# A four-layer graph network on one core: a negated sigmoid gate, one selection per stretch, and a stream of adjacency pieces in other memory

## The chip, the cores and the metric

The kernel runs on one core of a Trainium2 chip. The core has four compute engines with a queue each: TensorE (PE: matrix products; its weight loads are listed as PEld), VectorE (DVE), ScalarE (ACT) and GpSimd (POOL). SyncE (SP) computes nothing here and issues most of the transfers. Every engine works through its own instructions in order and waits for others through semaphores. Transfers between HBM and the on-chip memory run on 16 DMA engines, whichever queue issued them.

The metric is the device time of one execution in microseconds. Before the change it is 3158.1 us, the median of 17 runs between 3150.41 and 3168.55.

## What is computed

There are 3125 nodes with 128 features, and 50000 edges sorted by destination. Four graph layers follow each other, each with a residual and a layer norm:

```python
edge_index = jnp.stack([src, dst])
x = _layernorm(x + _L0_gnn_ref(x, edge_index, edge_weight, ...))      # 3 GCN layers with relu
x = _layernorm(x + _L1_gnn_ref(x, edge_index, ...))                   # GATv2 attention, 4 heads
x = _layernorm(x + _L2_gnn_ref(x, edge_index, edge_attr_128, ...))    # CGConv
x = _layernorm(x + _L3_gnn_ref(x, edge_index, edge_weight, ...))      # 10 GCN layers, LN, GELU, residual
```

Each GCN layer computes D^-1/2 (A + I) D^-1/2 (x W) + b. The part that the change rewrites most is layer 2, which works on edges:

```python
z = jnp.concatenate([x[dst], x[src], edge_attr], axis=-1)
gate = jax.nn.sigmoid(z @ W_f + b_f)
core = jax.nn.softplus(z @ W_s + b_s)
agg = jax.ops.segment_sum(gate * core, dst, num_segments=x.shape[0])
return x + agg
```

## The kernel before, in words

**Dense products (layers 0 and 3).** The kernel builds the dense adjacency matrix in HBM, as 7 banks of 460 columns by 25 row tiles of 128. A GCN layer is then a product of the node features with these banks. `Convolutions.sums` (line 657 loads, line 691 multiplies) goes over a bank in pieces of five row tiles, 128x5x460 floats or 1150 KB each. Some pieces stay on chip (`adj`), the others pass through a stream of buffers (`adj_k`). Five matmuls use one piece. When the 25 matmuls of a bank are done, its sums are evicted to `aggT`, and a later product with the layer's weights (`po`, line 708) gives the new rows.

**Layer 0 and the building of the adjacency.** `l0_sorted` builds the banks from one-hot matrices on PE (`heavy`, `side`), collects each bank in a `strip`, stores it (line 562), and runs the first GCN layer from the strips on the way. Two memory pools serve this: `l0_strips` and `l0_hot` (the one-hots), opened in this order. When they are closed, the stream `l0_adj` with four buffers and `l0_hold` take their place; a tile in memory that others used must wait for the last reader of those. Then `load_nodes` (line 147) loads x again and `Attention.prepare` (lines 1077 to 1137) loads and computes the index tables of layer 1: zeros stored to HBM, the padded destinations `dst_pad`, `wide`, `order`, `src_o`. All these transfers are on SP's queue, as are the pieces `adj_k`.

**Layer 1** goes over the edges in 28 stretches of 14 chunks of 128 edges. A stretch has four blocks, of 4, 4, 3 and 3 chunks (`BLOCKS`). For each chunk POOL gathers 128 rows by an indirect transfer (line 217). The gathered rows of a stretch are one tile `xj`, with six buffers.

**Layer 2** (`l2_sorted`, from line 1362) first computes two tables, one row per node (lines 1440 to 1470): `to_src`, the product with the source part of the weights, and `to_dst`, that with the destination part plus the bias, in three bf16 parts. `w2` and `b2` hold the weights and biases of gate (index 0) and core (index 1). Then it goes over the same 28 stretches:

- `load(s)`: SP loads `xw` (the stretch's own node rows), POOL gathers the fourteen chunks of `zj`, a tile per stretch, three buffers.
- `load_block(s, b)`: SP loads `td` (42 consecutive rows of `to_dst`, three parts each), `eaT` (edge features) and `drow` (each edge's local destination, broadcast over 126 partitions), four blocks ahead.
- `select(s, b)`: DVE compares `drow` with the partition's number, which gives the one-hot `of_node`, two blocks ahead.
- `products(s, b)`: PE multiplies `eaT` by the weights and `of_node` by `td`, into `pz` in PSUM (three buffers).
- `soften`: DVE adds `zj` (z = pz + zj), ACT takes Abs. `soften_more`: ACT takes Exp(−|z|), then Ln(1 + that), back into `pz`.
- `gate_core`: DVE computes min(z, 0) − ln for the gate, ACT its Exp; DVE computes max(z, 0) + ln for the core.
- `messages`, `place`: DVE multiplies gate and core to `msg`, and builds the one-hot `of_edge`.
- `add_up(s)`: PE sums the messages by node, one matmul per chunk, and adds the carried part of the stretch before (`agg`, by `shift`). `rows(s)` copies the sums to `agg`, forms u = 2·xw + agg and its moments; `finish(s)` writes the normalised rows y and stores them to `after`.

While this goes on, layer 3's first GCN layer begins. After stretches 6, 12, 18 and 24 (`WHOLE`), `fetch` loads finished rows of x back and `scale` multiplies them by dinv on ACT. From stretch 7 on, each stretch takes one adjacency piece `adj_u` (`load_unit`, three buffers): `unit` multiplies it with five matmuls at the end of the stretch (b = 3), and `add_unit` adds the sums to `aggT` at the start of the next (b = 0). The last seven units come after the last stretch.

**Layer 3** then starts with its first product's remaining rows (the last five row tiles), with loads of bias and norm rows (`three`, line 1701, three buffers) on SP ahead of its pieces.

**The order of the work.** In layer 2 the order on PE, DVE, ACT and SP is written out: `InOrder` (helper, line 181, which records every instruction under line 189) chains each instruction to the one before on its engine. The loop at lines 1634 to 1675 steps through all blocks, k = 4s + b, and calls the functions above for different blocks at each step. Only POOL's gathers and the operations outside of `InOrder` are placed by the scheduler.

Of the kernel before, what the change touches and what calls it, by code (L numbers as in the profile page):

```python
# [18 lines left out]
P = 128  # L19
D = 128  # L20
# [28 lines left out]
def tile_gnn_stack(ctx: ExitStack, tc: tile.TileContext, a: dict, out: bass.AP):  # L49
# [96 lines left out]
    def load_nodes():  # L146
        nc.sync.dma_start(x, a["x"].rearrange("(t p) d -> p t d", p=P))
# [635 lines left out]
    def l0_sorted(edges, adj, attention):  # L783


        with (
# [13 lines left out]
            with (  # L800
                tc.tile_pool(name="l0_strips", bufs=2) as strips,
                tc.tile_pool(name="l0_hot", bufs=2) as hot,
            ):
                lanes.pin()
                edges.build(strips, hot, ps, adj, lambda b, strip: conv.sums(x, b, *layers[0], strip), ready)
                lanes.free()
            with (
# [3 lines left out]
                load_nodes()  # L811
# [249 lines left out]
    class Attention:  # L1061
# [15 lines left out]
        def prepare(self, scratch, ps, ve):  # L1077
# [11 lines left out]
            nc.sync.dma_start(self.left[NP:].rearrange("p a b -> p (a b)"), zero)  # L1089
            zero_f = scratch.tile([P, D], F32, name="zero_f")  # L1090
            nc.vector.memset(zero_f, 0.0)
            nc.sync.dma_start(self.before[NP:], zero_f)
            nc.sync.dma_start(self.after[NP - P:NP], zero_f)
            nc.sync.dma_start(self.logits[:, :NEAR], zero_f[:HEADS, :NEAR])
            nc.sync.dma_start(self.logits[:, NEAR + NCH * P:], zero_f[:HEADS, :NEAR])
            edge = scratch.tile([1, NEAR + 1], I32, name="edge")
            nc.vector.memset(edge, NP)
            nc.sync.dma_start(dst_pad[:, :NEAR + 1], edge)
            nc.sync.dma_start(dst_pad[:, NEAR + 1 + NCH * P:], edge)
            v = a["dst_r"]  # L1100
            nc.sync.dma_start(dst_pad[:, NEAR + 1:NEAR + 1 + NCH * P],
# [4 lines left out]
            nc.sync.dma_start(wide, bass.AP(tensor=dst_pad.tensor, offset=dst_pad.offset,  # L1106
# [6 lines left out]
            nc.sync.dma_start(order, bass.AP(tensor=v.tensor, offset=v.offset,  # L1113
                                             ap=[[SC, P], [SE, NS], [1, SC]]))
            v = a["src_r"]
            nc.sync.dma_start(self.src_o.rearrange("p (s c) -> p s c", c=SC), bass.AP(
# [52 lines left out]
    def l1_sorted(at):  # L1169
        right, left, before, after, local, logits = at.right, at.left, at.before, at.after, at.local, at.logits  # L1170
        fresh, src_o, dl, att, bias, apart, step = (at.fresh, at.src_o, at.dl, at.att, at.bias, at.apart, at.step)
        with (
# [6 lines left out]
            with (  # L1179
# [13 lines left out]
                def load(s):  # L1193
# [8 lines left out]
                    t["xj"] = one.tile([P, SC, D], F32, name="xj", bufs=6)  # L1202
                    for c in range(SC):
                        gather(t["xj"][:, c, :], right, src_o, s * SC + c)
# [6 lines left out]
                def inputs(s, b):  # L1211
# [3 lines left out]
                    for c in range(n):  # L1215
                        pe_.matmul(zT[:, c * P:(c + 1) * P], t["xj"][:, c0 + c, :], ident, is_transpose=True,
# [59 lines left out]
                def messages(s, b):  # L1276
                    t, (c0, n) = st[s], BLOCKS[b]
                    if b == 0:
# [4 lines left out]
                                  t["xj"][:, c0:c0 + n, :].rearrange("p c (h d) -> p (c h) d", d=HD),  # L1283
# [78 lines left out]
    def l2_sorted(conv):  # L1362
# [10 lines left out]
        with (  # L1373
# [56 lines left out]
            for s, name in enumerate(("L2_gnn_b_f", "L2_gnn_b_s")):  # L1430
                v = a[name]
                nc.scalar.dma_start(b2[:, s, :], bass.AP(tensor=v.tensor, offset=v.offset, ap=[[0, P], [1, D]]))
            eps = one.tile([P, 1], F32, name="eps")
# [35 lines left out]
            with (  # L1469
# [16 lines left out]
                def load(s):  # L1486
                    t = st[s]
                    t["first"] = first_of(s)
                    t["xw"] = two.tile([P, D], F32, name="xw")
                    sp.dma_start(t["xw"], before[bass.ds(t["first"], P)])  # L1490
                    t["zj"] = zj.tile([P, SC, 2 * D], F32, name="zj")
                    for j in range(SC):
                        gather(t["zj"][:, j, :], to_src, src_i, s * SC + j)

                def load_block(s, b):
# [9 lines left out]
                    t["drow", b] = drow = ahead.tile([3 * FEW, 4 * P], BF16, name="drow", bufs=5)  # L1505
                    sp.dma_start(drow[:, :n * P], bass.AP(
                        tensor=local.tensor, offset=local.offset + e0, ap=[[0, 3 * FEW], [1, n * P]]))

                def select(s, b):
                    t, n = st[s], BLOCKS[b][1]  # L1510
                    t["of_node", b] = of_node = ahead.tile([3 * FEW, 4 * P], BF16, name="of_node", bufs=4)
                    ve.tensor_scalar(of_node[:, :n * P], t.pop(("drow", b))[:, :n * P], third[:3 * FEW], None,
# [306 lines left out]
```

## Time and profile before

| stretch of time | what runs | length us | PE busy us | DVE busy us |
|---|---|---|---|---|
| 60 to 347 | adjacency is built, first layer of layer 0 | 287 | 258.43 | 242.10 |
| 347 to 371 | between the first and second layer | 24 | 8.77 | 6.87 |
| 371 to 660 | second and third layer | 289 | 283.18 | 53.59 |
| 660 to 1203 | layer 1 | 543 | 405.30 | 350.77 |
| 1203 to 1283 | tables of layer 2 | 80 | 33.41 | 33.77 |
| 1283 to 1409 | stretches without adjacency pieces | 126 | 98.87 | 113.88 |
| 1409 to 1823 | stretches with adjacency pieces | 414 | 338.84 | 347.94 |
| 1823 to 1869 | last units, entry of layer 3 | 46 | 29.40 | 9.48 |
| 1869 to 3158 | layer 3 | 1289 | 1272.87 | 443.86 |

The span is 3158.1 us and the profiled execution took 3160.22 us, so 2.1 us lie outside of the span. The stages were cut by hand at the first and last instructions of their functions; busy times are those of the instructions inside. Where an engine is busy for nearly the whole length, it is the bound of that stage. Where none is, the chain of waits has to be followed.

### The profile page before, as it was taken

To read this page: it belongs to the slowest core of one execution; us is meant where nothing else is said; L and a number is where in the kernel's file an instruction comes from. 1 tells how busy PE (TensorE), PEld (TensorE's weight loads), DVE (VectorE), ACT (ScalarE), POOL (GpSimd) and SP (SyncE) were. 2 spreads that over 40 slices of the span, in tenths; PEclk is the share of its full clock that TensorE was granted. 3 is DMA by queue.
4 is the path that set the end of the run, shared out by engine and by line. 5 is a ranking of instruction groups with operands and counts; after the bars stand their busy time and mean duration, and the time that the engine had idled before them with its cause. 6 is when DMAs were issued, how large, how long until landed. Compare 5 with 4: busy or idle time off the path is not lost.

```text
span 3158.1 us, 33089 instructions
## 1 busy us (share of the span) xinstructions
PE 2744.8 (87%) x11223; PEld 1585.5 (50%) x11223; DVE 1643.9 (52%) x4368; ACT 989.4 (31%) x1491; POOL 822.6 (26%) x864
## 2 busy tenths in 40 slices
PE   2899799967877774678888879999999999999997
PEld 2666455533443343456556545555555555555554
DVE  7999101226776675788888836522222332222234
ACT  1333000123333332667767614311111111211121
POOL 4211000047777752676666300000000000000000
PEclk8999899978888887789989989999999999999999
DMA  2354787733333325778887684666666676666765
GB/s 63 118 174 164 256 301 252 244 106 99 103 107 102 107 85 174 208 230 247 240 246 241 190 281 164 221 213 218 221 209 228 216 232 208 226 217 207 229 216 165
DMA packets 413151, 609.90 MB, mean 193 GB/s; under 512 B 55434, under 2 KB 380312, under 8 KB 412956
## 3 DMA queue, kind: packets, MB, share of 16 engines
q1 hardware_dynamic: 366094, 520.33, 50.8%
q0 software_dynamic: 32320, 79.09, 8.8%
q10 hardware_dynamic: 14558, 8.27, 0.9%
q8 instruction: 91, 1.49, 0.2%
q14 instruction: 88, 0.72, 0.1%
HBM read 545.16 MB, written 62.61 MB: 192 GB/s over the span
## 4 chain that ended last, share of the span: by engine, by line
PE 64%; DVE 11%; DMA 10%; POOL 9%; issue 4%; ACT 2%; SPq 1%; DVEq 0%; another core or an unknown queue 0%; POOLq 0%; ACTq 0%
PE acc L691 46%; POOL xj L217 8%; PE sums L189 4%; PE acc L189 4%; PE pz L189 3%; DMA drow<-s_local 3%; PE side L189 2%; PE po L708 2%; DVE heavy L189 2%; POOL zj L217 2%; DMA xj<-s_right,src_o 1%; DVE msg L189 1%; DVE z L189 1%; DMA zj<-s_to_src,src_i 1%; DMA s_to_dst<-parts 1%
## 5 line engine op out<-in xcount | busy, mean ns | idle before, releaser
L691 PE MATMUL acc<-adj_k,xs 128*128 128x460 f32 (+1 forms) x2920 | 1121.2, 538 | 3.0 <-DMA adj_k<-bank 3.0
L691 PEld LDWEIGHTS acc<-adj_k,xs 128*128 128x128 f32 x2920 | 548.2, 190 | 502.7 <-issue 450.4
L217 POOL DMA_INDIRECT xj<-s_right,src_o x392 | 374.6, 956 | 458.0 <-ACT parts L1162 338.8
L217 POOL DMA_INDIRECT zj<-s_to_src,src_i x392 | 373.4, 953 | 206.2 <-issue 110.0
L691 PE MATMUL acc<-adj,xs 128*128 128x460 f32 (+1 forms) x1000 | 393.9, 544 | 16.4 <-DMA adj<-bank 16.4
L189 PE MATMUL pz<-w,eaT 128*128 128x256 f32 x784 | 258.9, 430 | 127.4 <-DVE msg L189 102.2
L724 DVE SCALAR_TENSOR_TENSOR v<-po,dinv,three 128x128 f32<-128x128 f32 x250 | 72.4, 344 | 476.6 <-PE po L708 476.4
L691 PEld LDWEIGHTS acc<-adj,xs 128*128 128x128 f32 x1000 | 190.5, 191 | 204.0 <-issue 192.2
L189 PEld LDWEIGHTS pz<-w,eaT 128*128 128x128 f32 x784 | 135.3, 213 | 200.3 <-DVE msg L189 124.5
L736 ACT ACTIVATE rs<-rs 128x4 f32<-128x4 f32 (+2 forms) x91 | 18.6, 205 | 682.8 <-DVE rs L735 682.6
L189 PEld LDWEIGHTS sums<-msg,of_edge 128*128 128x128 f32 x1568 | 204.4, 212 | 45.5 <-DVE of_edge L189 20.7
L189 PE MATMUL sums<-msg,of_edge 128*128 128x132 f32 (+1 forms) x1568 | 211.3, 298 | 12.2 <-DVE msg L189 12.2
L189 PE MATMUL zT<-ident,xj 128*128 128x128 f32 x392 | 100.5, 324 | 116.0 <-DMA xj<-s_right,src_o 115.0
L189 PEld LDWEIGHTS <-heavy 128*128 128x128 bf16 x1875 | 122.5, 102 | 81.8 <-issue 58.4
L189 PEld LDWEIGHTS zT<-ident,xj 128*128 128x128 f32 x392 | 50.5, 147 | 217.7 <-DMA xj<-s_right,src_o 156.5
L1710 ACT ACT_TABLE_LOAD x77 | 98.8, 1283 | 192.7 <-DVE v L1709 192.6
L189 PE MATMUL acc<-strip,x 128*128 128x460 f32 (+1 forms) x350 | 157.1, 557 | 0.0
L189 PE MATMUL side<-of_pair,heavy 128*128 128x125 bf16 x1875 | 134.9, 226 | 24.3 <-DVE heavy L189 19.6
L189 ACT ACTIVATE leaky<-zT 128x512 f32<-128x512 f32 (+1 forms) x112 | 60.6, 541 | 277.1 <-PE zT L189 263.8
L189 ACT ACTIVATE strip<-side 128x500 f32<-128x500 f32 (+1 forms) x157 | 91.4, 586 | 159.5 <-PE side L189 158.2
L189 DVE TENSOR_TENSOR heavy<-of_low,columns 128x2560 bf16<-128x2560 bf16 (+1 forms) x96 | 139.2, 1505 | 1.0
L189 ACT ACTIVATE soft<-z 128x1024 f32<-128x1024 f32 (+1 forms) x112 | 106.2, 948 | 85.3 <-DVE z L189 85.3
(220 smaller groups left out, 3319.5 us busy)
## 6 DMA issues: line engine op xcount, KB each, us to landing
adj_k<-bank SPq DMA_DIRECT2D x246, 1150.0 KB
adj_k<-bank SPq DMA_DIRECT2D x46, 912.5 KB
bank<-strip SPq DMA_DIRECT2D x6, 5750.0 KB
adj_u<-bank SPq DMA_DIRECT2D x24, 1150.0 KB
adj<-bank SPq DMA_DIRECT2D x14, 1150.0 KB
eaT<-in_ea_t SPq DMA_DIRECT2D x56, 256.0 KB
drow<-s_local SPq DMA_DIRECT2D x28, 448.0 KB
eaT<-in_ea_t SPq DMA_DIRECT2D x56, 192.0 KB
```

The costliest lines, as they stand in the source:

```text
L189: ins = getattr(self.engine, name)(*args, **kwargs)
L217: after_writers(nc.gpsimd.indirect_dma_start(out=to, out_offset=None, in_=table[:NP, :], in_offset=bass.IndirectOffsetOnAxis(ap=index[:, c ...
L691: lanes.tensor.matmul(acc[:, :c1 - c0], xs[:, t, :], k[:, q, :c1 - c0], start=(t == begin), stop=(t == NT - 1))
L708: lanes.tensor.matmul(po[:, t - t0, :], self.aggT[:, t * P:(t + 1) * P], w, start=True, stop=True)
L724: lanes.vector.scalar_tensor_tensor(to[:, t - t0, :], sums[:, t - t0, :], dinv[:, t:t + 1], bias, op0=OP.mult, op1=OP.add)
L736: nc.scalar.activation(rs[:, :n], rs[:, :n], AF.Sqrt)
L1710: nc.scalar.activation(v, v, AF.Gelu)
```

## The change

The text below holds what the change does, in the order of the code.

- In `l0_sorted` the pool of the one-hots is opened before that of the strips, so that the stream which follows lies in the one-hots' memory. `load_nodes` there, and the transfers of `Attention.prepare`, are issued by ACT's queue.
- In both edge layers the gathered rows have a tile for each block: `xj` with 22 buffers, `zj` with 10.
- In layer 2 the gate's weights and bias are negated, once. The gate is then Exp(−(max(z, 0) + ln)), so one DVE instruction over both halves serves gate and core, and ACT's Exp has a scale of −1.
- `drow` is loaded and compared once per stretch, for all 14 chunks, with one buffer for `drow`. `select(s + 1)` stands at b = 2 of stretch s, the load at b = 0, ahead of `xw`.
- `agg` is copied by ACT, and u reads the sums in PSUM.
- A unit is multiplied in two parts: three matmuls at b = 3 as before, the last two at b = 0 of the next stretch; its sums are added at b = 1.

```diff
-    def load_nodes():
-        nc.sync.dma_start(x, a["x"].rearrange("(t p) d -> p t d", p=P))
+    def load_nodes(queue=nc.sync):
+        queue.dma_start(x, a["x"].rearrange("(t p) d -> p t d", p=P))
...
             with (
+                tc.tile_pool(name="l0_hot", bufs=2) as hot,
                 tc.tile_pool(name="l0_strips", bufs=2) as strips,
-                tc.tile_pool(name="l0_hot", bufs=2) as hot,
             ):
...
-                load_nodes()
+                load_nodes(nc.scalar)
...
-            nc.sync.dma_start(self.left[NP:].rearrange("p a b -> p (a b)"), zero)
+            nc.scalar.dma_start(self.left[NP:].rearrange("p a b -> p (a b)"), zero)
...
-            nc.sync.dma_start(wide, bass.AP(tensor=dst_pad.tensor, offset=dst_pad.offset,
+            nc.scalar.dma_start(wide, bass.AP(tensor=dst_pad.tensor, offset=dst_pad.offset,
                                             ap=[[SC, P], [SE, NS], [1, SPAN + 2]]))
...
-                    t["xj"] = one.tile([P, SC, D], F32, name="xj", bufs=6)
-                    for c in range(SC):
-                        gather(t["xj"][:, c, :], right, src_o, s * SC + c)
+                    for b, (c0, n) in enumerate(BLOCKS):
+                        t["xj", b] = one.tile([P, 4, D], F32, name="xj", bufs=22)
+                        for c in range(n):
+                            gather(t["xj", b][:, c, :], right, src_o, s * SC + c0 + c)
...
+            nc.vector.tensor_scalar_mul(w2[:, :, 0, :], w2[:, :, 0, :], -1.0)
+            nc.vector.tensor_scalar_mul(b2[:, 0, :], b2[:, 0, :], -1.0)
...
                     t["first"] = first_of(s)
+                    t["drow"] = drow = two.tile([3 * FEW, SE], BF16, name="drow", bufs=1)
+                    sp.dma_start(drow, bass.AP(tensor=local.tensor, offset=local.offset + s * SE,
+                                               ap=[[0, 3 * FEW], [1, SE]]))
...
-                    t["zj"] = zj.tile([P, SC, 2 * D], F32, name="zj")
-                    for j in range(SC):
-                        gather(t["zj"][:, j, :], to_src, src_i, s * SC + j)
+                    for b, (j0, n) in enumerate(BLOCKS):
+                        t["zj", b] = zj.tile([P, 4, 2 * D], F32, name="zj", bufs=10)
+                        for j in range(n):
+                            gather(t["zj", b][:, j, :], to_src, src_i, s * SC + j0 + j)
...
-                    t["drow", b] = drow = ahead.tile([3 * FEW, 4 * P], BF16, name="drow", bufs=5)
-                    sp.dma_start(drow[:, :n * P], bass.AP(
-                        tensor=local.tensor, offset=local.offset + e0, ap=[[0, 3 * FEW], [1, n * P]]))
-
-                def select(s, b):
-                    t, n = st[s], BLOCKS[b][1]
-                    t["of_node", b] = of_node = ahead.tile([3 * FEW, 4 * P], BF16, name="of_node", bufs=4)
-                    ve.tensor_scalar(of_node[:, :n * P], t.pop(("drow", b))[:, :n * P], third[:3 * FEW], None,
-                                     op0=OP.is_equal)
+
+                def select(s):
+                    t = st[s]
+                    t["of_node"] = of_node = two.tile([3 * FEW, SE], BF16, name="of_node")
+                    ve.tensor_scalar(of_node, t.pop("drow"), third[:3 * FEW], None, op0=OP.is_equal)
...
-                    ve.scalar_tensor_tensor(gate[:, :n], z[:, :n, :D], 0.0, soft[:, :n, :D],
-                                            op0=OP.min, op1=OP.subtract)
-                    ac.activation(gate[:, :n], gate[:, :n], AF.Exp)
-                    ve.scalar_tensor_tensor(soft[:, :n, D:], z[:, :n, D:], 0.0, soft[:, :n, D:],
-                                            op0=OP.max, op1=OP.add)
+                    ve.scalar_tensor_tensor(soft[:, :n], z[:, :n], 0.0, soft[:, :n], op0=OP.max, op1=OP.add)
+                    ac.activation(gate[:, :n], soft[:, :n, :D], AF.Exp, scale=-1.0)
...
-                    ve.tensor_copy(agg, t["sums"])
+                    ac.activation(agg, t["sums"], AF.Copy)
...
-                    ve.scalar_tensor_tensor(u, t["xw"], 2.0, agg, op0=OP.mult, op1=OP.add)
+                    ve.scalar_tensor_tensor(u, t["xw"], 2.0, t["sums"], op0=OP.mult, op1=OP.add)
...
-                    if b == 0 and s - 1 - FIRST in sums_of:
+                    if b == 1 and s - 1 - FIRST in sums_of:
                         add_unit(s - 1 - FIRST)
...
-                    if b == 1 and s + 1 < NS:
+                    if b == 0 and s + 1 < NS:
                         load(s + 1)
...
+                    if b == 0 and s - 1 - FIRST in sums_of:
+                        unit(s - 1 - FIRST, room, range(3, CK))
...
-                    if k + 2 < len(steps):
-                        select(*steps[k + 2])
+                    if b == 2 and s + 1 < NS:
+                        select(s + 1)
...
                     if b == 3 and FIRST <= s < NS:
-                        unit(s - FIRST, ps_s.tile([P, 512], F32, name="sums"))
+                        room = ps_s.tile([P, 512], F32, name="sums")
+                        unit(s - FIRST, room, range(3))
```

## The prediction, made before the result was known

> **What bounds the kernel now.** I read the page's totals first, then the chain of work that ended last, then the busy times by stage, and for the stages that the change touches the waits, the groups of instructions by shape and the timeline.
>
> ```profile
> PE 64%; DVE 11%; DMA 10%; POOL 9%; issue 4%; ACT 2%; SPq 1%; DVEq 0%; another core or an unknown queue 0%; POOLq 0%; ACTq 0%
> ...
> 347.00:371.00 24.00, 8.77 (x23) 4.31 (x22) 6.87 (x15) 0.48 (x1) 0.00 (x0) 0.64 0.93 259
> 371.00:660.00 289.00, 283.18 (x858) 152.60 (x858) 53.59 (x185) 24.66 (x70) 0.00 (x0) 1.00 0.78 261
> ...
> 1283.00:1409.00 126.00, 98.87 (x494) 70.93 (x494) 113.88 (x231) 91.58 (x123) 87.31 (x92) 0.85 0.73 211
> 1409.00:1823.00 414.00, 338.84 (x1700) 240.22 (x1701) 347.94 (x719) 285.43 (x405) 247.89 (x263) 0.93 0.77 230
> 1823.00:1869.00 46.00, 29.40 (x100) 16.39 (x99) 9.48 (x23) 2.49 (x5) 0.00 (x0) 0.86 0.84 272
> ```
>
> Each row of the stage table is start:end, length, then busy time of PE, PEld, DVE, ACT, POOL, the granted clock, the DMA share and GB/s. Where dense products run (371 to 660, and 1869 to 3158 with PE busy 1272.87 of 1289) PE is the bound and the change leaves it alone. Three other places matter. Between 347 and 371 PE stands almost idle. In layer 2's stretches DVE is busiest (113.88 of 126, then 347.94 of 414), the others close behind. Between 1823 and 1869 PE waits again. The chain names what ends last there:
>
> ```profile
> 347.19 8.64 DMA x<-in_x
> 358.66 12.53 DMA adj_k<-bank
> 371.24 21.10 PE acc L691 x54
> ...
> 1486.96 10.84 DMA drow<-s_local
> ...
> 1845.39 10.08 DMA three<-in_L_gnn_ln_g
> 1855.55 13.11 DMA adj<-bank
> ```
>
> **1. The gap at 347.** SP's queue holds load_nodes (347.19, let go by layer 0's last matmul) and prepare's transfers up to 358.66 before three of the pieces adj_k; matmul 6 starts at 371.24, and from there PE runs without a gap. After, the stream lies in the one-hots' memory, last read by the side matmul that ends at 327.4, so the compiled order puts piece 1 ahead of the last bank's store (328.46) and pieces 2 to 4 right behind it; x and prepare's small loads go through ACT's queue. Piece 1 then is there when PE ends the first layer (po at 347.66), its five matmuls take 3.86 us as in the steady state (6.31 in the cold gap), and matmul 6 stands at 352: 19 us earlier. Against that: a piece of 1150 KB takes 3.5 us alone (estimate: 261 GB/s at a share of 0.78 is 335 GB/s), x and wide are 3 MB or 9 us of the same transfers, and they start at 347 too. From 342.5, when the store's transfers end, to 347 one piece and a third pass alone; then they share, a piece in 7 us against 3.86 of matmuls, until some 364: PE slips 3 us. ACT's queue also holds wide behind dst_pad, and layer 1's evictions stand behind it; the first is due 19.3 us after block 0 starts, at 367, when wide has been issued (before, it went out 11 us after x: 358 if the same here). Sum −16; ends −8 (the slip is all 9 us and 2 of eviction) and −20.
>
> A rule that speaks against this part: the Trainium skill, "DMA: Bandwidth & Descriptors", section "Issuing engines are not separate DMA queues", says that transfers started by different engines interleave on the same 16 DMA engines, so that a second issuer saves only sequencer time. The row beside it is the 0.93 DMA share in the gap, which agrees that the engines are full. By the rule alone the gain would be SP's ten issues, about 7.5 us; what it leaves out is that DMA has room before 347.
>
> **2. Layer 1's gathered rows.** 22 tiles of four chunks (5.5 stretches) take the place of 6 of fourteen. POOL issues 392 gathers of 0.956 us with 0.3 us of issue each from 673 to 1163, and the only long wait is the first 338.8 us. No wait for a buffer is shown, so none can go or come: 0 (ends −2, +3).
>
> **3. Layer 2's preparation.** Two multiplications by −1 on DVE (under 0.7 us each: the 128x512 rows of DVE take 0.68) stand ahead of the first products. The stage is paced by s_to_dst<-parts and its two buffers (ACT parts waits 19.2 us for it): 0 (−1, +3). At its end the first products waited for the first drow; now drow of stretch 0 is loaded much earlier and only td is left: −1.5 (−3, 0).
>
> **4. Layer 2's DVE work per stretch of 14 chunks.**
>
> Groups on DVE by shape (count, busy us, mean ns) and waits (us in total, times, longest):
>
> ```profile
> L189 DVE TENSOR_TENSOR z<-pz,zj 128x1024 f32<-128x1024 f32 x56 | 68.2, 1218 | 0.5 <-PE pz L189 0.4
> ...
> L189 DVE SCALAR_TENSOR_TENSOR pz<-z,pz 128x512 f32<-128x512 f32 x56 | 38.9, 695 | 1.9
> L189 DVE SCALAR_TENSOR_TENSOR gate<-z,pz 128x512 f32<-128x512 f32 x56 | 38.2, 682 | 4.8 <-ACT pz L189 3.4
> ...
> ACT xs L189 <- DMA x<-s_after: 27.0, 4, 7.5
> DVE msg L189 <- ACT gate L189: 24.2, 6, 6.9
> DVE of_node L189 <- DMA drow<-s_local: 19.0, 10, 4.0
> DVE columns L189 <- PE sums L189: 17.9, 12, 2.4
> ```
>
> Gate and core become one instruction over 1024 columns: 682+695 ns become 1218 (as z, the same size from the same places), for three chunks 544+562 become 954. The four selections (two of 384 ns, two of 338) become one of 1792 columns: 0.69, the time of layer 1's selection of that width. agg's copy (282) goes to ACT. Saved: 2×0.16+2×0.15+0.75+0.28 = 1.65 us of the 16.7 that one stretch takes from y to y before the adjacency work begins (DVE is hardly idle there). Twenty-eight times that is 46 us.
>
> But a loop tightens. Before, ACT's gate Exp needed only the first, 0.68 us, instruction. Now it waits for the whole 1.22; behind it on ACT, in order, stand the Exp and the Ln of the next block, and DVE's next merged instruction waits for that Ln: 1.22+0.61+1.04+1.03 and 0.12 for hand-over (an estimate) is 4.02 us for four chunks, 0.95+0.51+0.83+0.81+0.12 = 3.22 for three, 3.83 and 3.58 for the mixed ones. DVE's own blocks now take about 3.3, 3.4, 4.7 and 4.1. The larger of both at each block: 3.83+4.02+4.72+4.08 = 16.65. Gain per stretch 0 where I counted 1.65. I take the loop: 0 for the seven stretches before the adjacency (ends −12 and +3).
>
> **5. The selection's row and the adjacency stretches.** From stretch 7 on a stretch takes 19.3 us on average, 2.6 us above the bare one: it waits for drow, for the sums of the unit, for gates behind the four scalings. The change removes the wait for sums (17.9 us in 12): the unit's last two products and its addition come a block later, and 0.64 us of addition falls into the loop's idle time. It moves drow: one load of 448 KB at b = 0, behind the 1150 KB of adj_u, td and eaT on SP, with one buffer; the selection for the next stretch stands at b = 2 in DVE's order, so all behind it (place, msg, the next z) waits if it is late. Before, first drow after y could be seen 10.5 to 13.7 us after y, with 126 KB; now 325 KB more must land, 1.0 us at 335 GB/s: 12.1 (11.5 to 14.7). DVE gets there at y+10.1: 2 us of wait, then 6.5 to the next y, 18.6 a stretch. SP adds its own loop: xw waits for u of the stretch before, and td and eaT of the next blocks are now queued behind it: 18.9. So 19.3 becomes 18.9 over 17 stretches: −7 (ends: −45 if DVE's 15.1 and none of these waits set it to 16.7, +27 if drow shows at y+14, 20.9). The four with fetch keep ACT's wait for x (27.0) and the scalings with drow behind it: +0.8 each, +3 (−4, +6).
>
> POOL's gathers (ten blocks, 2.5 stretches, where there were three) are a floor of 14×1.25 = 17.5 a stretch; the last one ends at 1777, 53 us before the last product of the stretches, so a shorter lead costs 0 (up to +10).
>
> **6. The entry of layer 3.** Nine loads three occupy SP from 1842.92 to 1850.25, the adjacency piece goes out at 1855.55, PE idles 16.36 us to 1868.79. After, seven of the nine stand ahead of the stretches' end in SP's order, since their memory is that of gathered blocks already free. x, two threes, two adj_k and adj then leave from 1842; three pieces at 3.5 us and about 4 of start put the first product near 1859: −9 (−4, −12; the seven loads may hold adj_u back, +0 to +5).
>
> **Sum.** −16 + 0 − 1.5 + 0 − 7 + 3 − 9 = −30.5. The profiled execution took 3160.2 us (span 3158.1 and 2.1 outside), 2.1 over the median of 17 runs: 3160.2 − 30.5 = 3129.7, and I say 3129. A measurement tells about 0.2%, 6.3 us.
>
> **Rivals.**
> - *Layer 2 runs at DVE's new pace.* For it: DVE busiest, pz has three buffers, the loop is worth only if ACT stays in this order. Against: the loop is made of waits in program order. 1.65×28 and half of the 2.6×21 waits are 46+27 in place of 4, with the other parts 100 less: 3060 to 3100.
> - *The first gap hardly closes*, because x and wide take the transfers: −8 there, the rest as above: 3138.
> - *The other side: the row of one load per stretch becomes the bound.* Place: DVE's selection at b = 2 waiting for drow. Each us it lands later costs 21 us. From y+13.7 on (4.1 late where I have 2) it eats 1.5×21 = 31 us, all the gain; at y+14.2 the time is 3171. For it: chain pieces of drow of 7 to 10.8 us in most adjacency stretches; against: it is issued at the place of the old first block.
>
> **How the numbers follow.** My forecast (with the small-gap case) between 3100 and 3152: 0.60. Layer 2 at DVE's pace, below 3100: 0.13. Within 6.3 us of before: 0.07. Drow or the loop above what was gained: 0.20. So faster 0.73, same 0.07, slower 0.20. The range leaves a tenth on each side: 3085 (the DVE case nearly whole) to 3172 (the other side at y+14.2).
>
> **What would show it.** Right: PE's first adj_k matmul right behind po near 348 and short stalls until 365; DVE idle in front of the merged instruction, put down to ACT's Ln; of_node waiting for drow some 2 us in the adjacency stretches; first product of layer 3 near 1859 less the shift before it. Wrong: drow waits of 4 us, or stretches of 15 us, or PE starved up to 371.

## The result: 1.1 per cent slower

The changed kernel took 3194.4 us (median of 8 runs, 3183.41 to 3199.78), the kernel before 3159.7 (46 runs): a ratio of 1.0106, 95% interval 1.0095 to 1.0118, so 30 to 37 us lost where 31 less had been forecast. That holds on chips where the kernel before takes 3160 us. On three others it takes 3543 to 3559 us, and the change, measured on one of them, is faster there, 0.967; they come last among the experiments.

The spans of the two traces cut at the same landmarks show where it went. Unless it says the end, a part counts as ended when the instruction at its right edge starts. Matmul 51 is the first of the second bank of layer 0's second layer: the trace lists two records for each product, so 50 stand ahead of it. Bare stretches are those without an adjacency piece, y is the instruction that writes a stretch's normalised rows, and y+10 means 10 us after it starts.

| part | before us | after us | difference | forecast |
|---|---|---|---|---|
| start to the end of the first layer's matmuls | 347.1 | 346.2 | −0.9 | 0 |
| to matmul 51 of layer 0's second layer | 39.7 | 30.8 | −8.9 | −16 |
| to layer 1 (matmuls, unchanged) | 271.3 | 271.3 | 0 | 0 |
| layer 1, to the load of x | 544.6 | 546.8 | +2.2 | 0 |
| layer 2's tables, to the first pz | 79.1 | 75.3 | −3.8 | −1.5 |
| to the first y | 35.8 | 35.8 | 0 | 0 |
| four bare stretches (y to y) | 66.9 | 72.2 | +5.3 | 0 |
| twenty stretches with pieces | 402.0 | 440.4 | +38.4 | −4 |
| three more y | 45.6 | 45.5 | −0.1 | 0 |
| last units, to the end of the last one | 20.3 | 28.4 | +8.1 | 0 |
| wait for layer 3's first piece | 16.4 | 9.1 | −7.3 | −9 |
| layer 3 | 1289.3 | 1289.4 | +0.1 | 0 |

Outside of layer 2's stretches the change gained 10.5 us, where 26.5 had been forecast; the stretches lost 44 us. The chain of the changed kernel, and its waits between 1195 and 1902 us (in all, times, longest):

```profile
PE 68%; DMA 12%; DVE 9%; issue 4%; POOL 4%; ACT 1%; SPq 1%; another core or an unknown queue 0%; DVEq 0%; POOLq 0%; ACTq 0%
...
328.02 20.83 DMA adj_k<-bank
348.85 12.86 DMA s_left<-zero
361.73 4.23 DMA order<-in_dst_r
...
1427.58 10.92 DMA drow<-s_local
...
1449.24 11.41 DMA drow<-s_local
```

```profile
PE pz L189 <- DVE msg L189: 66.7, 12, 8.5
DVE of_node L189 <- DMA drow<-s_local: 51.9, 14, 6.7
...
DVE columns L189 <- PE sums L189: 19.2, 10, 3.6
...
DVE pz L189 <- ACT pz L189: 15.3, 35, 0.8
DVE u L189 <- ACT agg L189: 14.4, 15, 4.0
...
PE pz L189 <- DMA eaT<-in_ea_t: 14.4, 6, 3.8
```

DVE's wait for drow has grown from 19.0 to 51.9 us; PE waits for eaT, which it did not before; DVE's wait for ACT's Ln (`pz`) has grown from 3.4 to 15.3, and the one for ACT's copy of the sums (`agg`) is new. DVE's wait for the units' sums (`columns`), which the change was to remove, is as long as it was (17.9, now 19.2); only ACT's fell (13.8 to 5.0). One stretch with a piece, SP's queue from y to y (columns: start, duration, engine, line, operation, out<-in):

```profile
1489.79 0.36 SPq L189 DMA_DIRECT2D s_after<-y  x1
1490.20 0.43 SPq L189 DMA_DIRECT2D adj_u<-bank  x1
1491.41 0.39 SPq L189 DMA_DIRECT2D td<-s_to_dst  x1
1491.89 0.50 SPq L189 DMA_DIRECT2D eaT<-in_ea_t  x1
1492.45 1.46 SPq L189 DMA_DIRECT2D drow<-s_local  x1
1506.33 0.34 SPq L189 DMA_DIRECT2D xw<-s_before  x1
1507.23 0.38 SPq L189 DMA_DIRECT2D td<-s_to_dst  x1
1507.70 0.84 SPq L189 DMA_DIRECT2D eaT<-in_ea_t  x1
1509.30 0.38 SPq L189 DMA_DIRECT2D td<-s_to_dst  x1
1509.77 0.34 SPq L189 DMA_DIRECT2D eaT<-in_ea_t  x1
1510.87 0.38 SPq L189 DMA_DIRECT2D td<-s_to_dst  x1
1511.34 0.34 SPq L189 DMA_DIRECT2D eaT<-in_ea_t  x1
1511.92 0.36 SPq L189 DMA_DIRECT2D s_after<-y  x1
```

And DVE in the same stretch (the bracket is the idle time before the instruction, and what ended it):

```profile
1500.09 1.23 DVE L189 SCALAR_TENSOR_TENSOR pz<-z,pz 128x1024 f32<-128x1024 f32 x1 [0.45 <-ACT pz L189]
1504.32 0.73 DVE L189 TENSOR_SCALAR of_node<-drow,third 126x1792 bf16<-126x1792 bf16 x1 [3.00 <-DMA drow<-s_local]
...
1506.03 0.27 DVE L189 SCALAR_TENSOR_TENSOR u<-xw,sums 128x128 f32<-128x128 f32 x1
```

This is a ring of waits. drow goes out at 1492.45, behind 1150 KB of adjacency, and is used at 1504.3. Until then DVE stands at the selection, and u, which is behind it, comes at 1506.0. xw has two buffers, and the one that the next stretch needs comes free only with that u: SP has stood at it since 1493.9. Behind xw stand td and eaT of three blocks, then y's store, the next adjacency piece, and the next drow. So a late drow makes u late, a late u makes xw late, and a late xw makes the loads behind it late. The link back to drow is the weakest: over the sixteen ordinary stretches with pieces (those without a fetch) drow goes out 3.7 us after y, where the first block's drow went out 3.3 us after it before the change. Most of the delay lies between issue and use, 11.2 us where it was 9.0.

The kernel before stood at xw too, with only two blocks behind it. A bare stretch there, SP and then DVE:

```profile
1338.88 0.40 SPq L189 DMA_DIRECT2D drow<-s_local  x1
1346.27 0.36 SPq L189 DMA_DIRECT2D xw<-s_before  x1
```

```profile
1345.95 0.29 DVE L189 SCALAR_TENSOR_TENSOR u<-xw,agg 128x128 f32<-128x128 f32 x1
```

SP's waits at that place, 1283 to 1900 us, before and after (they are put down to `st`, DVE's instruction behind u):

```profile
SPq L189 <- DVE st L189: 205.8, 26, 10.5
```

```profile
SPq L189 <- DVE st L189: 300.1, 26, 15.1
```

### The profile page after: what moved, and what is told of

It reads as the page before. It is cut to its first block, busy times and chain, and to the rows that moved or that the text cites. A ratio compares the mean times of both kernels' runs of the same rounds, so it can differ in the third digit from the quotient of the medians.

```text
span 3191.3 us, 32824 instructions
## 1 busy us (share of the span) xinstructions
PE 2751.8 (86%) x11223; PEld 1591.4 (50%) x11223; DVE 1613.1 (51%) x4146; ACT 997.2 (31%) x1520; POOL 825.4 (26%) x864
## 4 chain that ended last, share of the span: by engine, by line
PE 68%; DMA 12%; DVE 9%; issue 4%; POOL 4%; ACT 1%; SPq 1%; another core or an unknown queue 0%; DVEq 0%; POOLq 0%; ACTq 0%
PE acc L691 46%; PE pz L189 6%; PE sums L189 5%; DMA drow<-s_local 4%; DMA xj<-s_right,src_o 3%; POOL xj L217 3%; PE acc L189 3%; PE po L708 2%; PE side L189 2%; DVE heavy L189 2%; PE zT L189 1%; PE e L189 1%; POOL zj L217 1%; DMA s_to_dst<-parts 1%; DMA adj_k<-bank 1%
## 5 line engine op out<-in xcount | busy, mean ns | idle before, releaser
L736 ACT ACTIVATE rs<-rs 128x4 f32<-128x4 f32 (+2 forms) x91 | 18.6, 205 | 681.4 <-DVE rs L735 681.3
L189 PEld LDWEIGHTS sums<-msg,of_edge 128*128 128x128 f32 x1568 | 203.9, 212 | 47.0 <-DVE of_edge L189 18.6
L1712 ACT ACT_TABLE_LOAD x77 | 98.8, 1283 | 193.6 <-DVE v L1711 193.4
L189 DVE TENSOR_TENSOR z<-pz,zj 128x1024 f32<-128x1024 f32 (+1 forms) x112 | 121.7, 1086 | 22.6 <-DMA td<-s_to_dst 11.2
```

The costliest lines, as they stand in the source:

```text
L189: ins = getattr(self.engine, name)(*args, **kwargs)
L736: nc.scalar.activation(rs[:, :n], rs[:, :n], AF.Sqrt)
L1712: nc.scalar.activation(v, v, AF.Gelu)
```

## The experiments

### One link of the ring at a time

Three buffers for xw take SP out of the ring:

```diff
-                    t["xw"] = two.tile([P, D], F32, name="xw")
+                    t["xw"] = two.tile([P, D], F32, name="xw", bufs=3)
```

> The changed kernel with three buffers instead of two for xw in layer 2, nothing else. In its trace SP stands at xw's load for some 9 us of each stretch (1346.6 to 1356.3), because the buffer comes free only when DVE has formed u of the stretch before, and td and eaT of the next three blocks stand behind it; PE then waits for eaT 3.0 to 3.8 us at the start of stretches. Theory Q (this queue is what made the stretches longer): stretches without adjacency pieces go from 17.5-18.7 us back to 16.7 and those with pieces from 21.3 towards 19, 25 to 45 us off the whole. Theory R (the one selection row per stretch, which lands 14 to 16 us after y, is what DVE waits for): the bare stretches gain 1 us each, 5 to 8 us in all, and those with pieces stay at 21 or get worse, since more transfers stand beside drow: 0 to -10 us in all. Theory G (the loop through ACT): 0.

Measured: 3151.3 us, ratio to the kernel before 0.9972 (0.9958 to 0.9985), 43 us below the changed kernel. All bare stretches take 17.1 us, the sixteen ordinary ones with pieces 19.4 on average where they took 21.3. drow now goes out 3.2 us after y instead of 3.7 and is used 9.7 us later instead of 11.2; why it lands sooner is not shown. Theory Q's figures hold, but for the bare stretches, which stay 0.4 us above its 16.7; R's, as stated, fall.

Loading drow ahead of the adjacency piece takes drow out of it (`load_drow` holds the lines on drow that stood in `load`):

```diff
...
+                    if b == 0 and s + 1 < NS:
+                        load_drow(s + 1)
                     if b == 0 and 0 <= s + 1 - FIRST and s < NS:
                         load_unit(s + 1 - FIRST)
...
```

> The changed kernel with the load of the next stretch's drow moved ahead of the adjacency piece at b = 0 on SP, still 448 KB and one buffer. Theory R: drow is issued 1 us after y instead of 3.5 and nothing of the 1150 KB is before it, so it is there before DVE comes to the selection (y+10), the waits of DVE for drow (51.9 us in 14) are gone, and stretches with pieces go from 21.3 to about 19: 30 to 45 us off the whole. Theory Q: the waits change their place (to eaT and td behind xw), 0 to -15 us. Theory G: stretches stay above 18.5 whatever lands, -10 to -25 us.

Measured: 3157.4 us, ratio 0.9999 (0.9987 to 1.0010), 37 below the changed kernel: theory R's figure. So each opening alone gives back about the whole loss, and neither wait can be called the cause without the other. An ordinary stretch takes 19.4 us with xw freed and 18.7 with drow early; with both waits in place it takes 21.3, 1.9 more than the longer of the two. The waits show what is left of each (layer 2, first of the kernel with xw freed, then of the one with drow early):

```profile
DVE of_node L189 <- DMA drow<-s_local: 28.5, 12, 3.2
```

```profile
PE pz L189 <- DMA eaT<-in_ea_t: 52.7, 18, 4.9
```

With xw freed, DVE still waits for drow, for about half as long. With drow early, DVE never waits for it, but SP still holds eaT back, in every second stretch: stretches of 17 to 18 and of 19 to 21.5 us alternate.

The selection by blocks, as before the change, with xw's load left where the change put it (drow's load and `select` are by blocks again, too):

```diff
...
-                    if b == 2 and s + 1 < NS:
-                        select(s + 1)
+                    if k + 2 < len(steps):
+                        select(*steps[k + 2])
...
```

> The changed kernel with the selection as before: one drow of 448 or 336 bytes-per-row blocks of four or three chunks and one comparison for each block, the rest of the change kept (xw still loaded at b = 0, merged gate, unit in two parts). Theory R: the whole loss of the stretches goes, 30 to 45 us off the changed kernel's time. Theory Q: blocks of drow now also stand behind xw on SP, so it stays as slow or gets slower: -10 to +15 us. Theory G: -10 to -25.

Measured: 3232.2 us, ratio 1.0235 (1.0218 to 1.0253): 38 slower than the changed kernel, more than twice theory Q's upper bound and against R. Even bare stretches take 20.9 us. SP there, over one of them:

```profile
1381.11 0.40 SPq L189 DMA_DIRECT2D drow<-s_local  x1
1391.67 0.36 SPq L189 DMA_DIRECT2D xw<-s_before  x1
1392.59 0.36 SPq L189 DMA_DIRECT2D td<-s_to_dst  x1
1393.04 0.36 SPq L189 DMA_DIRECT2D eaT<-in_ea_t  x1
1393.46 0.40 SPq L189 DMA_DIRECT2D drow<-s_local  x1
```

SP stands at xw from 1381.5 to 1391.7, and now the blocks' drow is behind it too. With no piece in the way a stretch is nearly 4 us longer (20.9 against the 17.1 of the kernel with xw freed, which however also has the single drow; the kernel before, with drow by blocks and xw one step later, took 16.7). So this line, which only moved, costs time of its own; that the single drow, issued ahead of xw, had softened it is how I read 18.0 against 20.9. Blocks of drow with three buffers for xw were not run.

The gate in two instructions again:

```diff
-                    ve.scalar_tensor_tensor(soft[:, :n], z[:, :n], 0.0, soft[:, :n], op0=OP.max, op1=OP.add)
-                    ac.activation(gate[:, :n], soft[:, :n, :D], AF.Exp, scale=-1.0)
+                    ve.scalar_tensor_tensor(gate[:, :n], z[:, :n, :D], 0.0, soft[:, :n, :D], op0=OP.max, op1=OP.add)
+                    ac.activation(gate[:, :n], gate[:, :n], AF.Exp, scale=-1.0)
+                    ve.scalar_tensor_tensor(soft[:, :n, D:], z[:, :n, D:], 0.0, soft[:, :n, D:],
+                                            op0=OP.max, op1=OP.add)
```

> The changed kernel with the merged DVE instruction split again in two (gate half first, then ACT's Exp of scale -1, then the core half), so ACT's gate Exp waits 0.68 us for DVE and not 1.22. Theory G (the merged instruction closes a loop DVE-ACT of 16.65 us a stretch): bare stretches become shorter by 0.5 to 1 us, and in all 10 to 25 us come off. Theories Q and R: DVE only gets 0.65 us a stretch more to do where something else is waited for: -3 to +10 us.

Measured: 3184.8 us, ratio 1.0084 (1.0067 to 1.0100), 10 below the changed kernel, at the low end of theory G. Three of the four bare stretches take 16.5 to 16.6 us, where with the merged instruction the shortest are 17.1. The merge saves DVE instructions and makes the stretch longer.

### Both links opened, and the gate split

> The changed kernel with three buffers for xw, drow ahead of the adjacency piece and the split gate, as in two calls on the slower chip, where it took 8 and 18 us less than the changed kernel. Where the kernel before takes 3160: ring and loop theory 3106 to 3122 (each mend alone gave 3151 and 3157); transfers as the limit: 3143 to 3160.

Measured beside the kernel before on one chip (3159.9 us): 3122.6 us, ratio 0.988 (0.986 to 0.990). Bare stretches are 16.5 us, ordinary ones with pieces 17.7 (before 18.7 to 19.2 in two traces, changed 21.3). Its list of waits has none of DVE for drow any more, and PE's for eaT is down to 17.7 us in 7 (52.7 in 18 with drow early alone). The four stretches with a fetch still take 24.0; there ACT waits for x:

```profile
DVE msg L189 <- ACT gate L189: 28.5, 5, 7.4
ACT xs L189 <- DMA x<-s_after: 28.4, 4, 7.5
```

The measured time lies just above the 3106 to 3122 of the ring and loop theories and far below the 3143 of the theory that transfers set the limit. Opening one link alone gave 37 to 43 us, the three edits together 72. The kernel with both mends and the merged gate was only run on the slower chips, so the split's own share with the ring open is not separated here.

### The blocks' tiles alone

> The kernel before with only the gathered rows in a tile for each block (22 of xj, 10 of zj), nothing else of the change. Where the kernel before takes 3160, POOL waits for no buffer in layer 1, so this part is worth nothing: 3158 to 3163 (the changed kernel's layer 1 was 2.2 us longer in its trace). On the slower chip (3558 before, 3446 changed, layer 1 of the changed kernel 727 us instead of 547): if the blocks' tiles are what the change gains there, most of the 113 us, 3440 to 3480, and a layer 1 near 725 us; if not, 3558.

Its edit is the two loops over BLOCKS of the change, put into the kernel before. Measured beside it: 3164.7 against 3159.9 us, ratio 1.0021 (1.0008 to 1.0033), 2 to 10 us slower, where 0 was forecast. The traces do not place it: between this kernel's and that of the kernel before on the same chip layer 1 differs by −2.8 us and the stretches with pieces by +2.5, while two traces of the kernel before alone differ by 5 us in layer 1 (544.6 and 549.7) and by 6 in those stretches.

> The kernel before, unedited, for its trace beside the others. On the slower chip the 400 us that it loses should stand in layer 1 (544.6 before) and layer 2; if the blocks' tiles explain the sign there, POOL waits in this trace for a buffer of xj, which it never did in the first one. Elsewhere: 3160.

Measured: 3160.7 us, a single run on a chip like the first, so it shows those differences between executions and nothing of the slower chips.

### The two edges

> The changed kernel with two orders mended at its edges. On ACT's queue, order's load and what is made of it stand ahead of the zeros: in the trace PE stood 4.7 us at 361.9 to 366.6 for the transposed products of order, which was queued behind s_left. On SP the nine loads three stand behind the last load of x: in the trace seven of them sat ahead of the adjacency units' last pieces, whose first took 10.6 us in place of 5.8. Expected by these two readings: matmul 51 of layer 0 comes 4 to 5 us sooner after the first layer's end (30.8 now), the last units end 7 to 8 us sooner after the last y (28.4 now), but the entry of layer 3 then waits 16 instead of 9 for its piece: -5 to -7 in all. If the stretch from the last y to layer 3 is set by the units' three buffers and not by the loads three, the second part shows no change.

> The changed kernel with order first on ACT's queue and the loads three behind x, layer 2 unmended. By the two readings: matmul 51 of layer 0 at 26 after the first layer's end instead of 30.8; the last units 20 us after the last y instead of 28.4, but layer 3's wait 15 to 16 instead of 9: 3187 to 3190, against 3194.

Its edit moves order's load and what is made of it ahead of the zeros in prepare, and ties the loads three behind the load of x:

```diff
...
+                    if fetched:
+                        follow(ins, fetched)
...
```

Both fell on slower chips: 3453.2 and 3442.8 us, ratios 0.9698 and 0.9722, no faster than the changed kernel's 0.9674 on such a chip. The two parts can be read all the same, since they hold no gather, and the changed kernel's figures there (29.6; 26.5 and 9.7) are near its own elsewhere (30.8; 28.4 and 9.1). Layer 0's gap: 36.0 in both, a miss; nothing was gained and the gap is longer. In the second of them:

```profile
364.50 6.68 ACTq L1089 DMA_DIRECT2D order<-in_dst_r  x1
```

```profile
383.74 0.57 DVE L1094 TENSOR_TENSOR dl<-order,first_f 128x392 f32<-128x392 int32 x1 [12.10 <-DMA order<-in_dst_r]
```

```profile
384.37 0.90 PE L1099 MATMUL side<-ident,dl 128*128 128x128 f32 x3 [9.31 <-DVE dl L1094]
```

order goes out first, but beside x and three pieces it takes 19 us to land (364.5 to 383.7); behind them it took 4.2, and 4.4 in the changed kernel on a slower chip. Its place in the queue was not what made it late. PE's products of it stand among the second layer's matmuls in the compiled order, and PE waits 9.3 us there instead of 4.7. Six kernels of this family whose order was not moved had 28.8 to 36.4 in this part on the slower chips, the five with order first 34.6 to 36.0, so the size of the loss is uncertain; that there is no gain is not.

Layer 3's entry: the last units took 19.9 us in both, and the wait for layer 3's piece 15.4 and 16.4; together 35.3 and 36.3, against 36.3 for the changed kernel on such a chip (26.5 and 9.7). Their place only decides which of the two waits the loads three lengthen. That reading was right, and so was its price.

Then they were taken off the path: two sets of three loaded before layer 2, the others behind layer 3's resident pieces, together with both mends of layer 2, the split, and order first.

> All together: both mends of layer 2, the split gate, order first on ACT's queue, and the first two sets of three loaded before layer 2 while the rest go behind layer 3's resident pieces. Expected from the parts: the kernel with both and the split, less 5 for order and 7 to 9 for the loads three, which now stand neither ahead of the units nor ahead of layer 3's first piece: 3095 to 3110.

> Both mends, the split, order first on ACT's queue, and the first sets of three loaded before layer 2, the rest behind layer 3's resident pieces. From the parts, where the kernel before takes 3160: 10 to 15 us less than the kernel with both and the split, matmul 51 of layer 0 at 26 us after the first layer's end instead of 30.8, the last units at 20 instead of 28 after the last y, layer 3's wait at 6 to 9.

> Both mends, the split gate, order first, and the loads three neither ahead of the units nor of layer 3's first piece. 3122.6 of the kernel with both and the split, less 5 for order and 7 to 10 at the entry of layer 3: 3107 to 3112.

The three runs had 21.0, 21.3 and 21.1 us for the last units and 6.6, 6.7 and 6.8 for the wait: 27.6 to 28.0 in place of 36.3, 8 us gained, as expected. Their whole times (3443.2, 3437.4 and 3416.1 us; ratios 0.9661, 0.9645 and 0.9654) say little beyond that, since they also hold order first, and the rest lies in layers 1 and 2 of slower chips.

### The slower chips

> The changed kernel with both: three buffers for xw, and the next stretch's drow loaded ahead of the adjacency piece. Each alone took some 40 us off (medians 3151.3 and 3157.4 against 3194.4), which says that the two waits hold each other up in one ring: drow late, selection late, u late, xw late on SP, td, eaT and the next drow late. With only xw freed, stretches with pieces take 19.2 us and DVE still waits 28.5 us for drow; with only drow early they alternate between 17.15 and 21 and PE waits 52.7 us for eaT. If the ring is the whole cause, both together bring nearly all such stretches to the 17.14 of the bare ones: 20 to 30 us below the better of the two, 3121 to 3132. If the adjacency pieces cost their time by the transfers themselves, it stays within 8 us of 3151.

> As the kernel with both, and the merged gate and core instruction split in two again. The loop theory: with nothing else late, the bare stretch of 17.14 us is the ring DVE merged instruction, ACT Exp, Exp, Ln, DVE; with the split it is 16.5 (as the split alone showed in its undisturbed stretches), 0.6 us on up to 24 stretches: 10 to 15 us below the kernel with both. If DVE's total is the bound, it gets 0.65 us a stretch slower instead: 10 to 18 above.

> The changed kernel itself once more, unedited. The four kernels before this one ran on a chip on which the kernel before took 3558 us and not 3160, with ACT standing some 290 us in layer 1 for something that is not in the trace, so they can only be set against the changed kernel if it runs beside them. Where the kernel before takes 3160: 3194, a ratio of 1.010. On the slower chip: all of its siblings there were 3 per cent faster than the kernel before, so 0.97 to 0.98 if what slowed that chip is what the change avoids, 1.01 if the mends made the difference.

> Three buffers for xw and drow ahead of the adjacency piece, as in the run before on the other chip. The ring theory: 20 to 30 us below each alone, 3121 to 3132 where the kernel before takes 3160, nearly all stretches with pieces at 17.1 to 18. If transfers set the stretches: within 8 us of 3151.

> The same with the merged gate and core instruction split. The loop theory: bare stretches of 16.5 instead of 17.14 and 10 to 15 us less than both alone. DVE's total as the bound: 10 to 18 us more.

> The changed kernel with both mends of layer 2 and the merged gate kept. Beside it, on a chip where the kernel before takes 3160, the same with the split gate took 3122.6. Loop theory: 10 to 15 us more than that, 3132 to 3138, and bare stretches of 17.14. DVE's total: 10 less, 3112.

These six runs, and the five on the edges above, stood beside a kernel before of 3557.9, 3558.9 and 3542.8 us. The changed kernel: 3445.8, ratio 0.9674 (0.9642 to 0.9707). With both mends: 0.9680, 0.9637 and 0.9675 (3443.7, 3431.9 and 3430.3 us). With the split as well: 0.9651 and 0.9628 (3437.5 and 3428.3 us). So none of the figures expected for the first chip can be read there: mends that took 72 us off take 8 to 18, about the width of the intervals, and the sign of the change itself is the other one. Layer 1 of the changed kernel takes 727 us there instead of 547, its first four bare stretches of layer 2 89.4 instead of 72.2, while layer 3 is the same (1289.3). The end of the first layer comes 16 us later too (362.5 against 346.2). Two waits of layer 1 in the kernel with both mends on such a chip, 700 to 1300 us:

```profile
ACT leaky L189 <- remote: 290.9, 29, 18.1
...
POOL xj L217 <- PE e L189: 108.1, 15, 26.8
```

ACT stands 291 us, up to 18 at a time, for something that the trace does not hold ("remote"), and POOL, which hardly waited for a buffer in layer 1 elsewhere (5.8 us in the changed kernel's first trace, 700 to 1150 us), waits 108 us for one of xj. That a buffer by the block comes free earlier would fit the changed kernel's gain there, but the kernel with the tiles alone was not run on such a chip, and the kernel before has no trace from one. Neither the cause of the slowness nor that of the other sign is shown.

## Why the prediction was wrong, point by point

**The gap at 347 (−16 forecast, −8.9).** Piece 1 was there as forecast: the first adj_k matmul starts at 346.08, right behind the first layer. The pieces' waits cost 0.86 and 1.84 us, 2.7 of the 3 allowed. What failed is the list of what PE executes there: prepare's transposed products stand between the matmuls, and PE waited 4.66 us for them, since order landed only at 366. The trace before had shown the same wait, longer (first line; the others are from after):

```profile
360.68 1.21 PE L1123 MATMUL side<-ident,dl 128*128 128x128 f32 x4 [11.86 <-DVE dl L1118]
```

```profile
350.96 1.81 PE L691 MATMUL acc<-adj_k,xs 128*128 128x460 f32 x4 [0.86 <-DMA adj_k<-bank]
...
357.81 4.13 PE L691 MATMUL acc<-adj_k,xs 128*128 128x460 f32 x10 [1.84 <-DMA adj_k<-bank]
...
366.61 0.90 PE L1123 MATMUL side<-ident,dl 128*128 128x128 f32 x3 [4.66 <-DVE dl L1118]
```

The prediction asked what stands behind wide on ACT's queue, and not who waits for order. The measured −8.9 still lies inside its ends (−8 and −20). From the rule of the Trainium skill ("DMA: Bandwidth & Descriptors", "Issuing engines are not separate DMA queues") the prediction had estimated 7.5 us of gain. That the measured gain lies near it is no proof of the rule: piece 1 came early by its place in memory, and no run here separates the memory from the second issuer.

**Layer 1 (0) and the tables (−1.5).** +2.2 and −3.8 in the traces. The first is within the 5 us by which two traces of the kernel before differ; from the load of x to the first y those two differ by 1.9, so the second is more than that, and more than the −3 allowed. The tiles alone measured +2 to +10 us, above the 3 allowed in layer 1, though not above the 10 allowed in layer 2.

**The loop through ACT (0 for the bare stretches).** The mechanism is right: with nothing else late a bare stretch takes 17.1 us with the merged instruction and 16.5 without. The size is off by half a microsecond: 16.65 was worked out, and the kernel before took 16.7. In the changed kernel DVE also waits for the sums' copy, which was moved to ACT's queue behind the Ln and still stands ahead of u:

```profile
1352.70 1.23 DVE L189 SCALAR_TENSOR_TENSOR pz<-z,pz 128x1024 f32<-128x1024 f32 x1 [0.45 <-ACT pz L189]
...
1356.36 0.29 DVE L189 SCALAR_TENSOR_TENSOR u<-xw,sums 128x128 f32<-128x128 f32 x1 [0.79 <-ACT agg L189]
```

That 0.79 was not in the forecast: u reads the sums in PSUM, yet in the trace it starts only after ACT's copy of them. What this copy adds by itself was not run; with the gate split and both links open DVE waits for it only twice (4.7 us). The changed kernel's own bare stretches took 18.0; the rest goes with xw freed (17.1 in all four) and mostly with drow early (17.1 to 17.4 in three of four).

**The adjacency stretches (−7 and +3; measured +38.4).** This is the step that failed. The prediction took drow as visible at y+12.1, which gave 18.6 us, and SP's own loop through xw as 18.9 us, each worked out with the other held fixed, and took the larger. Measured: drow is used at y+14.9 on average in the ordinary stretches, and they take 21.3 us. With xw freed drow was used at y+13.0 and the stretch took 19.4, 0.8 above the forecast for drow; with drow early it took 18.7, where 18.9 had been forecast for SP's loop; with both links open and the gate split, 17.7. So the terms were about right and the larger of the two was not: together they cost 1.9 us a stretch more than the longer one alone, and with xw's wait in place drow is used some 2 us later. The four stretches with a fetch, forecast 0.8 longer each, are 1.1 longer. The wait for the units' sums, counted as removed, did not go either (17.9 before, 19.2 after).

**The entry of layer 3 (−9).** The wait for the piece fell by 7.3 as forecast. The "+0 to +5" for seven loads held ahead of adj_u was taken at 0 and was 8: SP stood 14 us at the first of them, until 1852.71, and seven loads then went out ahead of the units' pieces. The piece that the last six units' products wait for took 10.59 us where it had taken 5.78. Which of the two cost how much was not separated; with the loads behind x both went, and the last units took 19.9 us.

```profile
1838.14 0.49 SPq L189 DMA_DIRECT2D adj_u<-bank  x1
1852.71 0.34 SPq L1703 DMA_DIRECT2D three<-in_L_gnn_res_b  x1
...
1856.60 4.26 SPq L189 DMA_DIRECT2D adj_u<-bank  x3
```

**The rivals.** The one on the other side, given 0.20, named the place (DVE's selection at b = 2 waiting for drow) and the price (21 us for each microsecond): from 3171 at y+14.2 it gives 3186 at y+14.9, 8 short of the measured time. (At y+13.7 DVE would be 3.6 us late, not 4.1, which belongs to y+14.2.) It had not asked what would make drow that late, and that the sum comes so close is in part luck, since it also counts gains at the edges that were not made. Its row against (drow is issued where the first block's was) nearly held, 3.7 us after y against 3.3; what came late was the landing, 11.2 us from issue to use against 9.0. That layer 2 would run at DVE's new pace, 15.1 us, is ruled out by the 17.1 us of bare stretches.

## What to carry to other kernels

Here a load that waited for a buffer held back everything behind it on its queue, so a line moved up by one step has to be costed with all that it now stands ahead of; a third buffer of 512 bytes a partition was worth 43 us. When two waits are worked out separately, look whether each one's end delays the other's start. Then the larger of the two is not the cost of both (21.3 us against 19.4 here), and opening either link can give back the whole loss. Merging two instructions on one engine saved nothing where another engine needed only the first of them.

## What the runs showed of the hardware that was not expected

- One load of order (128x28x14 integers, 14 in a row) landed in 4.2 and 4.4 us behind other transfers and in 19 us beside x and three pieces.
- The same kernel takes 3160 us on some chips and 3543 to 3559 on others, with layer 3 within 2 us of 1289 on both, and for the changed kernel 180 of the 251 us of difference in layer 1 (547 against 727); the ratio of the changed kernel to the one before went from 1.011 to 0.967 between them.
